# ScalarE fetches 16 table rows per step in three bunches instead of 12 in two; SyncE takes a tile every ten steps instead of eleven

## The chip, the cores and the metric

The kernel runs on one core of one Trainium2 chip. The metric is the device time of one launch in microseconds (us), as the median of several runs. In the names of the profile PE is TensorE (PEld its weight loads), DVE is VectorE, ACT is ScalarE, POOL is GpSimd and SP is SyncE. A name with a q behind it (ACTq, SPq) is the instruction queue of that engine, where instructions are listed that only issue transfers or set registers.

## The reference

The kernel computes a ranking model over 16384 samples in float32. Each sample has 69 item numbers and one label, all of them rows of a table with 100001 rows of 96 floats (384 bytes).

```
u  = emb[batch_user]                 # 16384 x 69 x 96
ql = emb[batch_label[:, 0]]          # 16384 x 96
z  = concat([q, u, q - u, q * u])    # q is ql repeated over the 69 fields
h  = dice(z @ W1 + b1, a1)           # 384 -> 64, dice(x) = (alpha * (1 - p) + p) * x, p = sigmoid(x)
att = (h @ W2 + b2) @ W3 + b3        # 64 -> 16 -> 1
pre = where(batch_user < 100000, u * att, 0)
pooled = einsum("gf,bfe->bge", window, pre)   # ten groups of fields
x = concat([pooled, ql])             # 11 * 96
y = dice(x @ Wf1 ...) -> dice(... @ Wf2 ...) -> ... @ Wf3    # 200, 80, 1
```

What matters here is the first line: 16384 x 69 rows must be fetched from the table by number.

## The kernel before, in words

The samples are worked on in 32 blocks of 512. A block's 512 x 69 items are cut into 69 chunks of 512 items: 64 "main" chunks (eight samples by 64 fields) and five "tail" chunks (512 samples, one of the last five fields each). A chunk is four tiles of 128 rows. Two chunks make a pair, and the kernel's unit of work is the pair: 1104 pairs, one per step of a plan that is written out by hand. `plan[step]` is a list of calls, and the order of the calls is the order in which the instructions stand in each engine's queue; no scheduler moves them.

What one step i does, in the order of the plan:

- sometimes `attend_rows` (every fourth step) and `spread` (every fourth step), which turn hidden values into attention weights;
- `hidden(i - 2)` (L399 and L403 on PE, L405 and L406 on ACT, L407 on DVE): the first layer and its dice;
- `scalar_rows(i, 0)`: a bunch of ScalarE's own row fetches, see below;
- `pool(i - 7)` (the group `acc<-rw,u` on PE, L470 on DVE): the weighted sums over fields;
- `fetch(i)`: for each of the pair's two chunks (j = 0 and 1) four tiles are fetched into the tile `u` and transposed by PE (`ptr<-ident,u`), DVE multiplies them by the label's row (L377), and ACT copies them out (L386, `uT<-ptr`);
- `scalar_rows(i, 1)`: the second bunch.

Beside that, the top layers of a finished block (L502 on PE and what follows) are spread over ten steps of the next block. The last eight steps and the end have an order of their own.

A tile's rows come in one of two ways. The usual one is `gather` (L266): one indirect transfer issued by GpSimd that fetches 128 rows by 128 numbers. The tile `u` has 14 buffers, and a pair's buffer is free when `pool` has read it, seven steps after its fetch.

The other way is the class `Singles`: 196 tiles are fetched row by row, 98 by SyncE and 98 by ScalarE, each row as one transfer of 384 bytes whose address is a register value (L301). Always the last tile (`SLOT = 3`) of a chunk is replaced. `SP_CHUNKS` and `ACT_CHUNKS` say which chunks; such a tile goes to a small ring (four buffers for SyncE, three for ScalarE), and PE waits for it by semaphore. `load` (L286) first loads a group of offsets into registers, 32 at a time on SyncE and 24 at a time on ScalarE. SyncE has nothing else to do and fetches a tile in one go. ScalarE fetches 12 rows in a step, for 11 steps per tile: six rows behind `hidden(i - 2)` (`half == 0`) and six behind `fetch(i)` (`half == 1`). The last of them stand three steps ahead of the step that reads the tile.

Of the kernel before, what the change touches and what calls it, by code (L numbers as in the profile page):

```python
# [48 lines left out]

ROW_BYTES = 4 * E  # L50
SLOT = 3
SP_CHUNKS = [2 * (11 * s + 9) + 1 for s in range(98)]
SP_RING = 4
ACT_CHUNKS = [2 * (11 * s + 15) + 1 for s in range(98)]
ACT_RING = 3
ACT_ROWS = 12
ACT_STEPS = -(-P // ACT_ROWS)
SINGLES = SP_CHUNKS + ACT_CHUNKS
NSB = (len(SINGLES) + P - 1) // P
# [3 lines left out]
def chunk_of(c):  # L63

    n, k = divmod(c, NCH)
    if n == NBLK - 1 and k >= EARLY:
        k = NMAIN + k - EARLY if k < EARLY + NTAIL else k - NTAIL
    return n, k
# [47 lines left out]
def rec_kernel(  # L116
# [158 lines left out]
    class Singles:  # L275
# [19 lines left out]
        def fetch(self, s, start, stop):  # L295

            b, k = self.buffers[s % len(self.buffers)], s % NSEM
            for r in range(start, stop):
                if r % self.group == 0:
                    self.load(s, r)  # L300
                d = self.engine.dma_start(  # L301
                    out=ring[r : r + 1, b], in_=row_bytes[:, bass.ds(self.values[r], ROW_BYTES)]
                ).then_inc(self.sems[k], 16)
                tc.no_tile_sem_insts.add(d.ins.name)
                tc.declare_no_dep(d.ins, group=f"ring{b}", reason="a buffer's readers have waited for its rows")
                fresh.setdefault(b, []).append(d.ins)
            if stop == P:
                for ins in fresh.pop(b):
                    tc.add_to_no_dep_group(f"ring{b}", ins)
                self.given[k] += 16 * P  # L310
                places[self.chunks[s]] = b, self.sems[k], self.given[k]
# [246 lines left out]
    def rows_of(b, n):  # L558
        return lambda: attend_rows(b, n)

    def spread_of(b, n):
        return lambda: spread(b, n)

    def pool_of(k):
        return lambda: pool(k)

    def hidden_of(k):
        return lambda: ys.__setitem__(k, hidden(k, *hs[k]))

    def tails_of(k):  # L570
        def work():
            uT = hs.pop(k)[0]
            for j in range(2):
                if chunk_of(2 * k + j)[1] >= NMAIN:
                    attend_tail(k, j, ys[k], uT)

        return work

    def fetch_of(k, between=()):
        def work():  # L580
            for j in range(2):
                n = chunk_of(2 * k + j)[0]
                if n not in pooled:
                    pooled[n] = bpool.tile([E, G, BLK], F32, tag="pooled", name=f"pooled{n}")
                    pres[n] = xpool.tile([E, NTAIL, BLK], F32, tag="pre", name=f"pre{n}")
            u, uT, quT = fetch(k, lambda: [w() for w in between])
            us[k], hs[k] = u, (uT, quT)

        return work
# [4 lines left out]
    def at(step, *work):  # L594
        plan.setdefault(step, []).extend(work)

    by_sync = Singles("sp", nc.sync, mybir.EngineType.SP, SP_CHUNKS, 0, range(SP_RING), 32)
    for s, m in enumerate(SP_CHUNKS):
        at(max(0, m // 2 - 6), lambda s=s: by_sync.fetch(s, 0, P))

    by_scalar = Singles(
        "act",
        nc.scalar,
        mybir.EngineType.Activation,
        ACT_CHUNKS,
        len(SP_CHUNKS),
        range(SP_RING, SP_RING + ACT_RING),
        2 * ACT_ROWS,
    )
    turn = {}  # L610
    for s, m in enumerate(ACT_CHUNKS):
        for k in range(ACT_STEPS):
            turn.setdefault(m // 2 - 2 - ACT_STEPS + k, []).append((s, k * ACT_ROWS, min(P, (k + 1) * ACT_ROWS)))

    def scalar_rows(i, half):

        for s, start, stop in turn.get(i, []):
            middle = min(stop, start + ACT_ROWS // 2)
            if half == 0:
                by_scalar.fetch(s, start, middle)  # L620
            elif middle < stop:
                by_scalar.fetch(s, middle, stop)

    c = NPAIR - CLOSE
    for i in range(c):
        if i >= 3 and (i - 3) % 4 == 3:
            at(i, rows_of(i - 6, 4))
        if i >= 3:
            at(i, tails_of(i - 3))
        if i >= 4 and (i - 4) % 4 == 3:  # L630
            at(i, spread_of(i - 7, 4))
        if i >= 2:
            at(i, hidden_of(i - 2))
        at(i, lambda i=i: scalar_rows(i, 0))
        if i < c - CLOSE:
            if i >= POOL_LAG:
                at(i, pool_of(i - POOL_LAG))
        else:

            for k in {0: (-15, -14), 1: (-13,), 3: (-12, -11), 4: (-10, -9), 7: (-8, -7)}.get(i - c + 8, ()):  # L640
                at(i, pool_of(c + k))
        at(i, fetch_of(i))
        at(i, lambda i=i: scalar_rows(i, 1))

    at(c, pool_of(c - 6), pool_of(c - 5), tails_of(c - 3), hidden_of(c - 2), fetch_of(c))
    at(c + 1, tails_of(c - 2), hidden_of(c - 1), fetch_of(c + 1))
# [113 lines left out]
```

## Time and profile before

| what | value |
|---|---|
| median of 3 runs | 10986.58 us (10983.78 to 10991.5) |
| the profiled execution's own time | 11010.73 us |
| its span, first to last instruction | 11009.0 us |
| granted TensorE clock, mean | 0.736 |
| gathers on POOL (L266) | 8764 (8636 of tiles `u`, 128 of labels) |
| rows fetched singly (L301) | 12544 on ACT, 12544 on SP |
| POOL busy, PE busy, ACT busy, DVE busy | 8291.3, 8954.4, 3169.5, 3006.0 us |

The busy times count an engine's work on data. Instructions that only issue a transfer or set a register are not counted as busy, so the single rows of ACT and SP (L301) and their offset loads (L286) are in none of these sums; they are seen in the rows of the engine's queue.

### The profile page before, as it was taken

What the parts mean: (1) busy time and instruction counts of PE and PEld (TensorE: products, weight loads), DVE (VectorE), ACT (ScalarE), POOL (GpSimd) and SP (SyncE); (2) the same over time, 40 slices, a digit from 0 to 9 for tenths busy, and PEclk for the clock granted to TensorE, in tenths of its full rate; (3) what the DMA queues carried; (4) which work ended last, traced back from release to release, by engine and by line L of the source; (5) the groups of instructions that cost most, each with busy time, mean ns of one, the idle gap of its engine ahead of it and who ended that gap; (6) DMA issues with size and microseconds to landing.
All of it is one profiled execution on the core that took longest, in us unless ns stands there. A gap on an engine that the chain in (4) does not pass through costs nothing.

```text
span 11009.0 us, 159604 instructions
## 1 busy us (share of the span) xinstructions
PE 8954.4 (81%) x41797; PEld 4357.6 (40%) x41797; DVE 3006.0 (27%) x5327; ACT 3169.5 (29%) x4969; POOL 8291.3 (75%) x8770
## 2 busy tenths in 40 slices
PE   7887888888887888878888878788788888888788
PEld 3333433333443333434433334334334334433335
DVE  3222222222222222222222222222222222222222
ACT  2222222222222222222222222222222222232223
POOL 7777777777777777777777777777777777777776
PEclk6767777677777777777777777777777776777777
DMA  2112111121111211112111121111212112111111
GB/s 49 41 41 43 41 41 41 41 43 41 41 41 41 43 41 41 41 41 43 41 41 41 41 43 41 41 41 41 43 41 41 41 41 43 41 41 41 41 41 35
DMA packets 333393, 457.69 MB, mean 42 GB/s; under 512 B 190594, under 2 KB 191106, under 8 KB 332354
## 3 DMA queue, kind: packets, MB, share of 16 engines
q0 software_dynamic: 280448, 431.33, 18.7%
q1 hardware_dynamic: 26946, 11.28, 0.4%
q10 hardware_dynamic: 25088, 4.87, 0.3%
q8 instruction: 336, 5.51, 0.2%
q14 instruction: 575, 4.71, 0.1%
HBM read 446.74 MB, written 0.07 MB: 41 GB/s over the span
## 4 chain that ended last, share of the span: by engine, by line
POOL 49%; issue 21%; PE 17%; DMA 12%; ACT 0%; DVE 0%; ACTq 0%; POOLq 0%
POOL u L266 48%; DMA u<-in_rows,ids 12%; PE p L502 4%; PE acc L325 3%; PE ph L399 2%; PE ph L403 2%; PE ptr L325 2%; POOL q L266 1%; PE prow L414 1%; PE pa L423 1%; PE ph L396 0%; PE ph L401 0%; PE pc L348 0%; PE patt L431 0%; PE p L513 0%
## 5 line engine op out<-in xcount | busy, mean ns | idle before, releaser
L266 POOL DMA_INDIRECT u<-in_rows,ids x8636 | 8169.4, 946 | 2635.4 <-issue 2429.3
L325 PE MATMUL ptr<-ident,u 128*96 128x128 f32 x8636 | 2015.9, 334 | 1962.7 <-DMA u<-in_rows,ids 1947.6
L386 ACT COPY uT<-ptr 96x512 f32<-96x512 f32 x2208 | 1267.4, 582 | 4384.7 <-DVE quT L377 3221.7
L325 PEld LDWEIGHTS ptr<-ident,u 128*96 128x96 f32 x8636 | 1154.4, 150 | 2736.8 <-DMA u<-in_rows,ids 2299.9
L325 PEld LDWEIGHTS acc<-rw,u 128*96 128x96 f32 x16018 | 1700.9, 189 | 1200.9 <-issue 1023.8
L407 DVE TENSOR_TENSOR y<-ph,y 128x512 f32<-128x512 f32 x1104 | 763.4, 691 | 4867.9 <-ACT y L406 4691.3
L377 DVE TENSOR_TENSOR quT<-ptr,qT 96x512 f32<-96x512 f32 x2048 | 1372.4, 677 | 1969.8 <-PE ptr L325 1967.9
L325 PE MATMUL acc<-rw,u 128*96 128x20 f32 x16018 | 1807.5, 260 | 37.5 <-DVE rw L436 31.8
L399 PE MATMUL ph<-uT,A 128*64 128x512 f32 x4096 | 1662.9, 889 | 1.0 <-ACT uT L386 1.0
L403 PE MATMUL ph<-quT,wn 96*64 96x512 f32 x4416 | 1601.4, 797 | 0.0
L405 ACT ACTIVATE y<-ph 128x512 f32<-128x512 f32 x1104 | 659.1, 597 | 2692.8 <-PE ph L403 2660.9
L406 ACT ACTIVATE y<-y,wn,na1c 128x512 f32<-128x512 f32 x1104 | 898.1, 814 | 37.2
L403 PEld LDWEIGHTS ph<-quT,wn 96*64 96x64 f32 x4416 | 441.1, 189 | 1050.7 <-issue 1049.6
L502 PE MATMUL p<-pooled,wf 96*100 96x512 f32 (+1 forms) x1400 | 679.4, 633 | 0.0
L399 PEld LDWEIGHTS ph<-uT,A 128*64 128x64 f32 x4096 | 266.0, 177 | 616.8 <-issue 612.1
L470 DVE COPY pooled<-acc 96x160 f32<-96x160 f32 x1008 | 420.6, 417 | 133.4 <-PE acc L325 133.4
L414 PE MATMUL prow<-y,v 128*32 128x512 f32 x2208 | 454.7, 900 | 1.0 <-DVE y L407 1.0
L502 PE MATMUL p<-pre,V 96*100 96x512 f32 (+1 forms) x700 | 401.3, 720 | 3.7 <-DVE x L485 3.4
L502 PEld LDWEIGHTS p<-pooled,wf 96*100 96x100 f32 x1400 | 256.1, 195 | 327.6 <-issue 327.6
L436 DVE SCALAR_TENSOR_TENSOR rw<-patt,bb,wn 128x320 f32<-128x320 f32 x554 | 277.5, 542 | 210.1 <-PE patt L431 206.6
L416 ACT COPY row<-prow 128x512 f32<-128x512 f32 (+1 forms) x277 | 161.9, 584 | 432.5 <-PE prow L414 402.1
L431 PE MATMUL patt<-ident,row 128*128 128x128 f32 x1108 | 221.6, 336 | 16.4 <-DVE pre L424 14.9
(72 smaller groups left out, 2438.5 us busy)
## 6 DMA issues: line engine op xcount, KB each, us to landing
ring<-in_rows SPq DMA_DIRECT2D x12544, 0.4 KB
ring<-in_rows ACTq DMA_DIRECT2D x12544, 0.4 KB
u<-in_rows,ids POOLq DMA_INDIRECT x8636
ids<-in_idx SPq DMA_DIRECT2D x8, 560.0 KB, 3.8
q<-in_emb,ids POOLq DMA_INDIRECT x128
wf<-in_far SPq DMA_DIRECT2D x1, 1209.0 KB, 6.4
wn<-in_near SPq DMA_DIRECT2D x1, 236.0 KB, 3.7
ids<-in_idx SPq DMA_DIRECT2D x1, 140.0 KB, 2.2
```

What stands on the lines that cost most here:

```text
L266: nc.gpsimd.indirect_dma_start(out=dst, out_offset=None, in_=table, in_offset=bass.IndirectOffsetOnAxis(ap=index, axis=0),)
L325: ins = op(out, ring[:, at[0]].bitcast(F32) if at else u[:, 4 * (c % 2) + t, :], other, **how)
L377: nc.vector.tensor_tensor(quT[:, j, :].rearrange("e (s f) -> e s f", f=FM), ptr.rearrange("e (s f) -> e s f", f=FM), by_field(q[:, k * NS ...
L386: nc.scalar.copy(uT[j][0:E], ptr)
L399: nc.tensor.matmul(p, As[n % 2][:, k // 4, :], uT[j], start=True, stop=False)
L403: nc.tensor.matmul(p, Wp, quT[:, j, :], start=False, stop=True)
L405: nc.scalar.activation(y, ph, AF.Sigmoid, scale=S_DICE)
L406: nc.scalar.activation(y, y, AF.Identity, bias=a1c, scale=na1c)
L407: nc.vector.tensor_mul(y, ph, y)
L414: nc.tensor.matmul(pr[32 * k : 32 * (k + 1), :], v2, ys[b + k], start=True, stop=True)
L470: nc.vector.tensor_copy(pooled[n][:, :, k * NS : (k + 2) * NS].rearrange("e g s -> e s g"), pa.rearrange("e j s g -> e (j s) g"),)
L502: nc.tensor.matmul(p1, w[:, h * DH : (h + 1) * DH], x, start=(k == 0), stop=(k == KTOP - 1))
```

## The change

ScalarE fetches 16 rows in a step instead of 12, so a tile takes eight steps instead of eleven, and it takes a tile every eight steps: 136 tiles instead of 98. Its tiles are now the last tile of the first chunk of a pair (j = 0) and no longer of the second. The 16 rows stand in three bunches: five behind `hidden(i - 2)`, five between the two chunks of `fetch(i)` (thus between the two copies of L386), and six behind `fetch(i)`. The loads of offsets grow with `2 * ACT_ROWS` from 24 to 32 values. SyncE takes a tile every ten steps instead of eleven: 109 tiles instead of 98. The rings, the gathers that remain and everything else stay.

```diff
-SP_CHUNKS = [2 * (11 * s + 9) + 1 for s in range(98)]
+SP_CHUNKS = [2 * (10 * s + 8) + 1 for s in range(109)]
 SP_RING = 4
-ACT_CHUNKS = [2 * (11 * s + 15) + 1 for s in range(98)]
+ACT_CHUNKS = [2 * (8 * s + 11) for s in range(136)]
 ACT_RING = 3
-ACT_ROWS = 12
+ACT_ROWS = 16
...
-    def scalar_rows(i, half):
+    def scalar_rows(i, third):
 
         for s, start, stop in turn.get(i, []):
-            middle = min(stop, start + ACT_ROWS // 2)
-            if half == 0:
-                by_scalar.fetch(s, start, middle)
-            elif middle < stop:
-                by_scalar.fetch(s, middle, stop)
+            by_scalar.fetch(s, start + third * ACT_ROWS // 3, start + (third + 1) * ACT_ROWS // 3)
...
-        at(i, fetch_of(i))
-        at(i, lambda i=i: scalar_rows(i, 1))
+        at(i, fetch_of(i, [lambda i=i: scalar_rows(i, 1)]))
+        at(i, lambda i=i: scalar_rows(i, 2))
```

## The prediction

> **What bounds the kernel now.** I read the page's busy times first, then who waited for whom on POOL and on PE, then the end of the chain. The page has PE busiest, but the waits say otherwise:
>
> ```profile
> PE 8954.4 (81%) x41797; PEld 4357.6 (40%) x41797; DVE 3006.0 (27%) x5327; ACT 3169.5 (29%) x4969; POOL 8291.3 (75%) x8770
> L266 POOL DMA_INDIRECT u<-in_rows,ids x8636 | 8169.4, 946 | 2635.4 <-issue 2429.3
> POOL u L266 <- issue: 2429.3, 7961, 0.3
> POOL u L266 <- PE ptr L325: 49.8, 163, 0.3
> PE ptr L325 <- DMA u<-in_rows,ids: 1947.6, 2358, 2.8
> PE acc L325 <- DVE rw L436: 31.8, 27, 3.0
> ```
>
> In the waits the numbers are us in total, times, longest. No gather waited longer than 0.3 us, and it did so before nearly every one: this is the gap of POOL's own issue. So a gather costs 0.946 us of work and 0.305 us (2635.4/8636) of gap, 1.251 us, and 8764 of them fill 10964 us: the first starts at 3.3 us, the last at 10967.05, a straight line. PE, in contrast, stood 1948 us waiting for gathered rows. POOL sets the pace and PE follows. (The chain of waits gives PE 17%; where it leaves POOL the gap is the same 0.3 us, so nothing was lost there.) The end of the chain:
>
> ```profile
> 10965.80 0.95 POOL u L266
> 10966.75 0.30 issue
> 10967.05 2.54 DMA u<-in_rows,ids
> 10969.59 0.04 issue
> 10969.63 0.32 PE ptr L325
> ```
>
> The last gather is followed by 42 us of PE, DVE and ACT work, which the change leaves alone. Time = 3.3 + 1.251 x gathers + 42.
>
> **The change part by part.**
>
> *Fewer gathers.* 109 + 136 tiles instead of 98 + 98 are 49 more outside POOL: 8715 gathers. Saved: 49 x 1.251 = 61.3 us, on the bound itself. In the profiled execution, span 11009.0, own time 11010.73, this gives 10949.4. The median is 24 us (0.22%) below that execution, so I scale: 61.2 us off 10986.6, 10925.4.
>
> *More rows on ACT: 136 x 128 = 17408, 4864 more.* They are covered by ACT's idle time, if it is long enough. The rows that price them:
>
> ```profile
> L301 ACTq DMA_DIRECT2D ring<-in_rows x12544: 213/213/566, 36.6 to 10740.7; - x200
> L286 ACTq TENSOR_LOAD <-offsets x588: 717/1678/1739, 34.8 to 10737.4; - x196
> L286 SPq TENSOR_LOAD <-offsets x392: 2023/2176/2396, 4.0 to 10309.1; - x196
> 5009.80 0.60 ACT L405 ACTIVATE y<-ph 128x512 f32<-128x512 f32 x1 [4.78 <-PE ph L403]
> 5010.43 0.81 ACT L406 ACTIVATE y<-y,wn,na1c 128x512 f32<-128x512 f32 x1
> 5012.25 2.01 ACTq L301 DMA_DIRECT2D ring<-in_rows  x6
> 5014.30 1.23 ACT L386 COPY uT<-ptr 96x512 f32<-96x512 f32 x2 [3.06 <-DVE quT L377]
> 5015.02 1.74 ACTq L301 DMA_DIRECT2D ring<-in_rows  x6
> 5017.62 0.60 ACT L405 ACTIVATE y<-ph 128x512 f32<-128x512 f32 x1 [2.09 <-PE ph L403]
> ```
>
> (Durations in ns are least/median/greatest; of the timeline, start and length in us.) Six rows take 1.74 us from the first one's start to the last one's end: 5 steps plus 0.213, so 0.305 us a row. Where SP issues too it is more; over the trace the mean distance of rows within a bunch is 0.326. A load of 32 offsets is priced by SP's row, 2.18 us, plus 0.25 because the first row behind a load takes 0.45 to 0.49 instead of 0.213.
>
> What ACT needs if it never waits for data, for two steps with one load: L406 stands behind L405 by 0.63, then its queue goes on while L406 and the copies run. Before: 2 x 0.63 + 1.68 + 0.25 + 24 x 0.305 = 10.5, or 5.3 us a step. After: 2 x 0.63 + 2.18 + 0.25 + 32 x 0.305 = 13.4, or 6.7 us. A step lasts 8715/1104 x 1.251 = 9.88 us. Even with nothing overlapped, ACT's sum is 3170 + 17408 x 0.326 + 544 x 2.43 = 10167 us of about 10950. So in the mean ACT keeps pace.
>
> [...]
>
> *What ACT's added time does to PE.* It adds 4 x 0.326 + 0.27 (loads: 544 x 2.43 less 98 x (5 x 1.68 + 0.72 + 6 x 0.25), over 1088 steps) = 1.6 us a step. At best nothing of it reaches PE. At worst all does, in 1088 steps: 1710 us, still below the 1948 us that PE waits for rows. The catch-up stretch above shows which is nearer: PE, behind by one step, went from one `pool` at 5009.69 to the next at 5017.49, 7.8 us, and ACT still waited 0.8 us for PE before the last L405. With 6.7 needed against 7.8, I take nearly nothing. The bunch between the two copies delays the second copy by up to 1.5 us; what is late next is PE's second transpose of the following step, a step away, and the hidden layer that reads `uT` two steps later.
>
> *How late may PE be?* POOL stalls only when `u` has no free buffer: 14 buffers, released seven steps after the fetch, so about 70 us. From the starts of the gathers and their transposes in the trace I worked out PE's lag: 2.5 us at least, 6.8 at the 75th percentile, at most 18.1 in blocks 0 to 30, and 32.5 at 10758 us in the last block. There remain 37 us.
>
> *The end.* There the lag counts directly: it falls from 23.7 us around 10843 to 3.0 at the last gathers, just in time. In the last 20 steps two or three tiles more are single (steps 1083, 1088, 1091; before, the last was at 1082), which brings POOL ahead of PE by 2.5 to 3.8 us, and ACT's rows now last to step 1088. Where PE doesn't follow, that part of the gain is lost, and up to 5 us more for ACT. Zero to 9 us; I take 2, because PE still waited 3.5 us for rows behind 10920.
>
> *At nothing:* SP's 1408 more rows. A tile takes some 50 us (74 rows in 29.22 us), every 99 us instead of 109; SP waited 5144 us for ring buffers. The ids that it loads on the same queue, 50 steps ahead, stay ahead. ACT's ring is read seven steps before its buffer is filled again (8(s-3)+18 against 8s+1), where it was 13. The queues' packets took 0.4% and 0.3% of the engines. The gather's pace has been 1.251 in the last 60 us too, where no rows are issued, so rows don't slow it. 49 more waits on PE are for tiles due two steps earlier.
>
> Sum: 10986.6 - 61.2 + 2 = 10927.
>
> **The rivals.** *PE's lag eats the gain in part.* If ACT's bunches add their full 1.6 us in the 20 steps of the last block where PE is behind, the lag there is 32 + 32 = 64 us, near the 70, and the end comes 10 to 30 us later: 10937 to 10957. Against it stands the 0.8 us of idle ACT in the catch-up stretch. *No gain:* PE becomes the bound everywhere. This needs over 1950 us of new waits on PE, more than everything that ACT adds; time 10965 to 11008. *Slower: ACT becomes the bound,* through the price of a row. Two queues issue closer together, and a row is slower when they meet (up to 0.566 us). [...] For it: the mean, 0.326, is above the quiet 0.305. Against: the waits of L386 and L405, 3222 and 2661 us before. *That the change doesn't reach POOL* is excluded by its count: 4 x 2208 - 245 + 128 = 8715.
>
> **How the numbers follow.** The forecast 0.80 (10920 to 10937), the partial gain 0.08, no gain 0.04, slower 0.08. The range holds the forecast's and most of the partial case: 10919 to 10948. About 0.2% is what a measurement of this kernel can tell from no change, 22 us. Faster 0.88, same 0.04, slower 0.08.
>
> **What would show it.** After: 8636 - 49 = 8587 gathers of `u`, 1.251 us apart, none with a wait over 0.3 us, span near 10950; 17408 and 13952 rows; ACT's rows still near 0.31 to 0.33 apart; PE still waiting over 1000 us for gathered rows, ACT's waits before L386 and L405 shorter by about 1500 together. Wrong if POOL waits for PE by whole microseconds, if PE waits for L386 instead of gathers, or if the tail behind the last gather is longer than 42 us by more than ten.

## The result and the profile after

The changed kernel takes 10925.1 us (median of 4 runs, 10924.09 to 10926.21), the kernel before 10987.9 us beside it: a ratio of 0.9943 with a 95% interval of 0.9926 to 0.996, or 62.8 us less (by the interval 44 to 81). The prediction was 10927, in a range of 10919 to 10948.

The busy times, the gathers and the last waits on POOL and PE (us in total, times, longest), of the changed kernel's profile:

```profile
span 10924.5 us, 172151 instructions
PE 8916.8 (82%) x41797; PEld 4347.4 (40%) x41797; DVE 2997.8 (27%) x5327; ACT 3181.0 (29%) x4969; POOL 8225.3 (75%) x8721
L266 POOL DMA_INDIRECT u<-in_rows,ids x8587 | 8103.7, 944 | 2619.7 <-issue 2455.0
POOL u L266 <- issue: 2455.0, 8047, 0.3
POOL u L266 <- PE ptr L325: 56.1, 184, 0.3
PE ptr L325 <- DMA u<-in_rows,ids: 1864.9, 2296, 2.7
PE acc L325 <- DVE rw L436: 41.9, 27, 4.6
PE ptr L325 <- ACT uT L386: 14.3, 17, 2.5
```

There are 49 gathers fewer, and still none of them waits over 0.3 us: POOL remains the bound and makes no pause but the 0.3 us ahead of each gather. PE waits 1865 us for gathered rows, 83 us less than before, and 14.3 us for ACT's copies. The added work on ACT, whose busy time does not show it, is in the rows of its queue (ns, least/median/greatest):

```profile
L301 ACTq DMA_DIRECT2D ring<-in_rows x17408: 213/213/527, 23.8 to 10747.0; - x198
L286 ACTq TENSOR_LOAD <-offsets x544: 2123/2182/2230, 21.5 to 10733.4; - x182
```

A row costs what it cost (a median of 213 ns in both profiles), and a load of 32 offsets costs on ACT what SP's row of before had shown (2182 ns against 2176). The three bunches in the timeline of ACT (start and length in us), in a step where the queue is behind:

```profile
8012.23 0.81 ACT L406 ACTIVATE y<-y,wn,na1c 128x512 f32<-128x512 f32 x1
8014.56 1.66 ACTq L301 DMA_DIRECT2D ring<-in_rows  x5
8016.26 0.58 ACT L386 COPY uT<-ptr 96x512 f32<-96x512 f32 x1 [3.22 <-issue]
8016.33 1.43 ACTq L301 DMA_DIRECT2D ring<-in_rows  x5
8017.80 0.58 ACT L386 COPY uT<-ptr 96x512 f32<-96x512 f32 x1 [0.96 <-issue]
8017.88 1.73 ACTq L301 DMA_DIRECT2D ring<-in_rows  x6
```

Between L406 and the first row stands the load of offsets (2.18 us, not listed among these lines). Both copies wait for "issue": PE had transposed their data by 8013.92, and the queue is still loading offsets and handing out rows. That is the price of the change on ACT, and little of it comes through to PE: the 14.3 us above.

The end of the span against the one before, in windows of the trace from the start of the last gather to the end of the span (us of the window, busy time and count of PE, PEld, DVE, ACT and POOL, the granted TensorE clock, DMA share, GB/s); first before, then after:

```profile
10967.10:11009.00 41.90, 34.63 (x227) 28.97 (x225) 7.22 (x18) 9.14 (x18) 0.90 (x1) 0.78 0.02 5
```

```profile
10885.40:10924.50 39.10, 32.63 (x231) 25.97 (x227) 7.18 (x18) 9.13 (x18) 0.94 (x1) 0.82 0.02 5
```

The tail became 2.8 us shorter with nearly the same instructions, at a higher granted clock (0.82, before 0.78).

### The profile page after: what moved, and what is told of

It reads as the page before. It is cut to its first block, busy times and chain, and to the rows that moved or that the text cites. A ratio compares the mean times of both kernels' runs of the same rounds, so it can differ in the third digit from the quotient of the medians.

```text
span 10924.5 us, 172151 instructions
## 1 busy us (share of the span) xinstructions
PE 8916.8 (82%) x41797; PEld 4347.4 (40%) x41797; DVE 2997.8 (27%) x5327; ACT 3181.0 (29%) x4969; POOL 8225.3 (75%) x8721
## 4 chain that ended last, share of the span: by engine, by line
POOL 51%; issue 23%; PE 15%; DMA 9%; ACT 1%; DVE 0%; ACTq 0%; POOLq 0%; DVEq 0%
POOL u L266 50%; DMA u<-in_rows,ids 9%; PE p L502 4%; PE acc L325 3%; PE ph L403 2%; PE ph L399 2%; PE ptr L325 2%; POOL q L266 1%; PE prow L414 1%; PE ph L396 0%; PE ph L401 0%; PE pa L423 0%; PE pc L348 0%; PE patt L431 0%; ACTq L301 0%
## 5 line engine op out<-in xcount | busy, mean ns | idle before, releaser
L386 ACT COPY uT<-ptr 96x512 f32<-96x512 f32 x2208 | 1283.4, 581 | 4630.3 <-DVE quT L377 2969.4
L325 PE MATMUL acc<-rw,u 128*96 128x20 f32 x15930 | 1812.3, 259 | 52.0 <-DVE rw L436 41.9
L405 ACT ACTIVATE y<-ph 128x512 f32<-128x512 f32 x1104 | 658.5, 596 | 2401.0 <-PE ph L403 2283.5
L406 ACT ACTIVATE y<-y,wn,na1c 128x512 f32<-128x512 f32 x1104 | 898.2, 814 | 36.7
L416 ACT COPY row<-prow 128x512 f32<-128x512 f32 (+1 forms) x277 | 161.6, 583 | 413.1 <-PE prow L414 305.4
```

Source lines behind the costliest of these rows:

```text
L325: ins = op(out, ring[:, at[0]].bitcast(F32) if at else u[:, 4 * (c % 2) + t, :], other, **how)
L386: nc.scalar.copy(uT[j][0:E], ptr)
L405: nc.scalar.activation(y, ph, AF.Sigmoid, scale=S_DICE)
L406: nc.scalar.activation(y, y, AF.Identity, bias=a1c, scale=na1c)
```

## The experiments

The theory of all of them: the time is 3.3 us, plus 1.249 us for each gather, plus a tail of about 40 us, as long as ScalarE, SyncE and PE keep pace. The rivals say that the added rows cost something, or that the bunches' places matter, or that the mean hides a bound that is near. Each kernel was timed beside the kernel before; differences below are against that run of before (10986.9 us in the first group, 10991.0 in the second, 10987.4 in the last).

**SyncE's part alone.**

```diff
-SP_CHUNKS = [2 * (11 * s + 9) + 1 for s in range(98)]
+SP_CHUNKS = [2 * (10 * s + 8) + 1 for s in range(109)]
-ACT_CHUNKS = [2 * (11 * s + 15) + 1 for s in range(98)]
+ACT_CHUNKS = [2 * (11 * s + 15) for s in range(98)]
```

> SyncE's part alone: a tile every ten steps (109 tiles), ScalarE as before (98 tiles, 12 rows in two bunches), but its tiles moved to the first chunk of the pair so that no tile is taken twice. 207 single tiles, 8753 gathers. Theory (the time is 3.3 us + 1.249 us x gathers + a tail of about 40 us, whatever fetches the other tiles): 11 gathers fewer, 13.7 us faster than before, about 10974. Rival (SyncE's denser rows slow the gathers or ScalarE's rows, where both issue): a gain clearly below 13.7, gathers more than 1.249 us apart.

Measured: 10973.5 us, 13.5 less, ratio 0.9987 (0.9977 to 0.9996). The gathers stand 1.249 us apart. The theory's 13.7 us is met to 0.2 us, closer than the interval (4 to 25 us less) can vouch for. (The second edit only moves ScalarE's tiles to the first chunk of the pair, so that no tile is taken twice.)

**ScalarE's part alone.** The changed kernel with SyncE's old line:

```diff
-SP_CHUNKS = [2 * (10 * s + 8) + 1 for s in range(109)]
+SP_CHUNKS = [2 * (11 * s + 9) + 1 for s in range(98)]
```

> ScalarE's part alone: 16 rows in three bunches, 136 tiles, SyncE as before (98). 234 single tiles, 8726 gathers. Theory: 38 gathers fewer, 47.4 us faster than before, about 10940. Rival (ScalarE's rows cost something that the larger saving hides): a gain clearly below 47, with POOL waits over 0.3 us or a longer tail behind the last gather.

Measured: 10940.3 us, 46.7 less, ratio 0.9956 (0.9939 to 0.9972). The two parts add up: 13.5 + 46.7 = 60.2 beside 62.8 and, in this group, 61.3 for the whole (the two-bunch form below).

**The rows without the gain.** In the changed kernel's `fetch`:

```diff
+AGAIN = set(SINGLES[::5])
...
                 if single(2 * i + j, t):
                     wait_for_single(2 * i + j, t)
-                else:
+                if not single(2 * i + j, t) or 2 * i + j in AGAIN:
                     gather(rows, u[:, 4 * j + t, :], ids[n][:, 4 * k + t : 4 * k + t + 1])
```

> The changed kernel with every fifth of its 245 single tiles gathered by GpSimd as well (into the place in u that nobody reads then): all the added rows, loads and bunches stay, and the number of gathers is again that of before, 8764. Theory (only the number of gathers counts, rows are free): the time of before, within 5 us of 10988. Rival (rows have a price that the change paid out of its 61 us): slower than before by that price; if ScalarE's added 1.6 us per step reached the path in the last block alone, by 10 to 30 us.

Measured: 10988.0 us, 1.0 more than before, ratio 1.0 (0.9991 to 1.001). The page's row of the gathers (a line was added, so it is L267 here):

```profile
L267 POOL DMA_INDIRECT u<-in_rows,ids x8636 | 8150.8, 944 | 2634.4 <-issue 2341.6
```

The number of gathers is that of before, and so is the time, with 6272 more rows in the queues. So the rows are free to within what this comparison can tell, some 10 us.

**Two bunches of eight.** The old `scalar_rows(i, half)` with `ACT_ROWS = 16`:

```diff
-        at(i, fetch_of(i, [lambda i=i: scalar_rows(i, 1)]))
-        at(i, lambda i=i: scalar_rows(i, 2))
+        at(i, fetch_of(i))
+        at(i, lambda i=i: scalar_rows(i, 1))
```

> The changed kernel, but ScalarE's 16 rows in two bunches of eight, behind hidden and behind fetch, as the 12 stood before, and none between the two copies. 8715 gathers. Theory (ScalarE has room, so the bunches' places do not matter to the time): 10925, the time of the changed kernel, with PE's lag behind the gathers at most a few us different. Rival (three bunches are what makes 16 rows affordable): slower than the changed kernel by 10 us or more, through L386 or L405 being late and a longer tail.

Measured: 10925.6 us, ratio to before 0.9943 (0.9927 to 0.996), the time of the three bunches. The largest lag of PE behind the gathers, worked out from the trace as in the prediction, is 26.5 us, with three bunches 26.8. At 16 rows a step the third bunch changes nothing that can be seen.

**ScalarE at 22 rows a step.** Here and below a third page of offsets takes 512 bytes per partition, and to make room for it SyncE's ring was given three buffers of 384 instead of four. Where a tile is not a whole number of steps (6 x 22 is more than 128), `scalar_rows` also cuts the last step short; that edit is left out below.

```diff
-SP_RING = 4
-ACT_CHUNKS = [2 * (8 * s + 11) for s in range(136)]
+SP_RING = 3
+ACT_CHUNKS = [2 * (6 * s + 9) for s in range(181)]
-ACT_ROWS = 16
+ACT_ROWS = 22
...
-        2 * ACT_ROWS,
+        32,
```

> ScalarE pushed further: 22 rows per step in three bunches (7, 7, 8), a tile every six steps (181 tiles), offsets still loaded 32 at a time; SyncE as in the changed kernel (109 tiles). SyncE's ring has three buffers instead of four, to make room for the longer table of offsets. 8670 gathers, 45 fewer than the changed kernel. By the prediction's sum ScalarE needs 0.63 + 22 x 0.324 + 22/32 x 2.43 = 9.4 us a step (9.0 at the quiet price of 0.305), and a step of POOL lasts 9.8. Theory (ScalarE still just keeps pace): 56 us faster than the changed kernel, 10869. Rival (the bunches fit in the mean but not in the steps with more work on ScalarE, so PE's lag grows to the end of u's buffers): POOL shows waits of whole microseconds, and the gain is below 40 us or gone.

Measured: 10874.2 us, 116.8 less than before (94 gathers fewer than before are 117.4), ratio 0.9894 (0.9877 to 0.991). PE's waits show how close ACT has come:

```profile
PE ptr L325 <- DMA u<-in_rows,ids: 769.8, 964, 2.0
PE ptr L325 <- ACT uT L386: 569.7, 358, 4.4
```

PE's wait for gathered rows is 770 us where the changed kernel had 1865: more than half of its spare time is gone, and its wait for ACT's copies rose from 14 to 570 us. POOL still never waits over 0.3 us for PE; PE's lag reaches 38.0 us of the 70.

**ScalarE at 26 rows a step.** The ring and the loads are as with 22 rows.

```diff
-ACT_CHUNKS = [2 * (8 * s + 11) for s in range(136)]
+ACT_CHUNKS = [2 * (5 * s + 8) for s in range(217)]
-ACT_ROWS = 16
+ACT_ROWS = 26
```

> ScalarE pushed past the point where the prediction's sum makes it the bound: 26 rows per step, a tile every five steps (217 tiles), the rest as with 22 rows. 8634 gathers. The sum is 0.63 + 26 x (0.305 to 0.324) + 26/32 x 2.43 = 10.5 to 11.0 us a step, more than POOL's 9.77. Theory (a row's price, not its number of bytes, decides when ScalarE becomes the bound): ScalarE sets the pace, 11400 to 11950 us, its waits before L386 and L405 nearly gone, and POOL waits for PE. Rival (ScalarE's queue hides more than the sum allows): 10825, POOL still without a wait.

Measured: 12355.6 us, ratio 1.1242 (1.1219 to 1.1264). The waits of POOL and PE:

```profile
POOL u L266 <- PE ptr L325: 1096.3, 432, 17.0
POOL u L266 <- PE acc L325: 559.6, 136, 13.7
PE ptr L325 <- ACT uT L386: 1541.4, 875, 6.2
```

PE's waits for gathered rows are nearly gone (27.9 us), PE waits for ACT, and POOL waits for PE, by up to 17 us at a time. PE's lag has a median of 75 us over most of the run, near the prediction's 70 us of buffers: `u` has none free. The mechanism is the one expected; the size is 400 us above the expected 11400 to 11950. A step took 12355.6/1104 = 11.2 us where the sum gave 10.5 to 11.0. The sum left out ACT's smaller work (L416, the top layers' dice L483 and L484, L349). Counted from the trace, the time in which ACT works or its queue hands something out is 10.5 us a step without that work, the low end of the sum, and 10.8 with it. For the other 0.4 us ACT stood still; why was not followed up.

**SyncE at a tile every six steps.**

```diff
-SP_CHUNKS = [2 * (10 * s + 8) + 1 for s in range(109)]
-SP_RING = 4
+SP_CHUNKS = [2 * (6 * s + 8) + 1 for s in range(181)]
+SP_RING = 3
```

> SyncE pushed: a tile every six steps instead of ten (181 tiles), ring of three buffers; ScalarE as in the changed kernel (136 tiles). 8643 gathers, 72 fewer than the changed kernel. SyncE needs about 50 us a tile of the 59 us that six steps last. Theory (only the number of gathers counts): 90 us faster than the changed kernel, 10835. Rival (two queues of single rows get in each other's way: rows of ScalarE at more than 0.33 us, or SyncE's tiles late, so that PE waits for the ring): clearly less than 90.

Measured: 10841.2 us, 149.8 less than before (121 gathers fewer are 151.1), ratio 0.9865 (0.9848 to 0.9881). SyncE is the cheaper place for more tiles: beside its rows and their offsets its queue has only the loads of item numbers and the stores of the result.

**Both.** The lines of the last and of the 22 rows together.

> Both pushed: ScalarE 22 rows per step and a tile every six steps (181 tiles), SyncE a tile every six steps (181 tiles), rings of three buffers each. 8598 gathers. Theory: 146 us faster than the changed kernel, 10779. Rival: where rows of both queues meet they cost more than 0.324, and ScalarE's sum (9.4 of 9.72 us per step) has no room for it: from 0.34 us a row on ScalarE is the bound, and the gain is smaller than that of SyncE's part alone (10835).

Measured: 10854.1 us, ratio 0.9872 (0.9855 to 0.9888): 12.9 us slower than SyncE's part alone, with 45 gathers fewer. The theory (10779) fails by 75 us, and the rival's sign came. Waits of POOL and PE, and the window behind the last gather:

```profile
POOL u L266 <- PE ptr L325: 66.2, 141, 6.7
PE ptr L325 <- ACT uT L386: 961.1, 535, 4.4
10771.40:10856.80 85.40, 72.17 (x468) 50.47 (x466) 23.65 (x49) 24.70 (x43) 0.91 (x1) 0.83 0.01 3
```

The gathers finished early, at 10771 us, but the last transpose began 50.7 us behind the last gather, where 2.5 us is usual. ACT had hardly any room left (0.63 + 22 x 0.334 + 1.67 = 9.6 us of a step of 9.72, before its smaller work). PE fell behind over the whole run, from a median lag of 9 us in the first sixteenth of the gathers to 58 in the last, and what it was behind is paid in the tail.

**19 rows a step, with SyncE every six steps and every five and a half.** The loads of offsets are as with 22 rows.

```diff
-SP_CHUNKS = [2 * (10 * s + 8) + 1 for s in range(109)]
-SP_RING = 4
-ACT_CHUNKS = [2 * (8 * s + 11) for s in range(136)]
+SP_CHUNKS = [2 * (6 * s + 8) + 1 for s in range(181)]       # the other: 2 * (11 * s // 2 + 8) + 1, 197 tiles
+SP_RING = 3
+ACT_CHUNKS = [2 * (7 * s + 10) for s in range(155)]
-ACT_ROWS = 16
+ACT_ROWS = 19
```

> ScalarE at 19 rows per step (6, 6, 7), a tile every seven steps (155 tiles), and SyncE a tile every six steps (181 tiles), rings of three buffers. 8624 gathers. ScalarE's sum is 0.63 + 19 x 0.33 + 19/32 x 2.43 = 8.3 us of a step of 9.75, where 22 rows needed 9.5 of 9.72 and left no room. Theory: 19 gathers fewer than SyncE's part pushed alone (10841), 10817, POOL without a wait over 0.3 us, a tail behind the last gather of about 40 us. Rival (ScalarE's last steps make PE late at the end even with room in the mean): a tail of 45 to 85 us, so no gain over 10841.

> As the one with 19 rows per step, and SyncE a tile every five and a half steps (197 tiles). 8608 gathers. SyncE needs 51 us a tile of the 53.5 us that its steps last. Theory: 16 gathers fewer again, 10797. Rival (SyncE is now the late one: PE waits for the ring's tiles, and with rows of both queues meeting all the time ScalarE's rows cost more): PE shows waits at L325 for rows of the ring, and the time is above 10817.

Measured: 15848.8 and 16582.6 us, but the kernel before took 13552.4 us on that chip, so neither theory can be judged by these two runs. The rows of the queues in the first of them:

```profile
L301 SPq MOVE ring<-in_rows x23168: 1/29/1481, 6.7 to 15644.5; - x200
L301 ACTq MOVE ring<-in_rows x19840: 2/29/1473, 99.7 to 15616.4; - x199
```

A register move of a row, which takes 30 ns at most in the traces from other chips, took up to 1.48 us there. Both kernels were run again on another chip.

> The kernel with 19 rows per step on ScalarE and a SyncE tile every six steps again, because in its first run the kernel before took 13552 us beside it, 2560 more than in every other comparison, so that nothing can be read from it about the gathers. 8624 gathers. Theory: beside a kernel before at 10987, 10817. Rival (the loss lies in the kernel, not in that chip): over 10987 here too.

> The kernel with 19 rows per step on ScalarE and a SyncE tile every five and a half steps again, for the same reason. 8608 gathers. Theory: 10797. Rival (SyncE's 51 us a tile do not fit 53.5 where both queues meet): PE waits for rows of the ring, above 10817.

Measured: 10815.2 us (ratio 0.9843, 0.9826 to 0.9859) and 10795.9 us (ratio 0.9827, 0.981 to 0.9843), 172.2 and 191.5 us less than before; the theory has 140 x 1.249 = 174.8 and 156 x 1.249 = 194.8. PE's waits in the second one:

```profile
PE ptr L325 <- DMA u<-in_rows,ids: 1669.9, 2006, 3.1
PE ptr L325 <- ACT uT L386: 71.5, 59, 4.9
```

PE waits for gathers again and hardly for ACT, so three rows a step fewer than 22 (and a tile every seven steps) give ACT its room back. The version with 19 rows and 5.5 steps is the fastest of all that were tried, 1.2% below the changed kernel.

## Why the prediction was right, point by point

*POOL sets the pace.* Shown: in every kernel in which ACT had room, and even with 22 rows, the median follows the number of gathers to within 3.3 us, from 11 to 156 fewer, and giving the 49 gathers back gave the time back.

*61.2 us for 49 gathers.* Right. The page of before has gathers of 946 ns and that of after 944. Over 8764 gathers 2.24 ns (945.98 less 943.74, from the trace) are 20 us, most of the 24 us by which the profiled execution of before stood above its median. So this part of the difference between the two profiled spans (84.5 us) belongs to no edit; scaling to the median was the right step.

*ACT's added rows are hidden.* Right, and shown to some 10 us by the run with the rows but without the gain. The price was right too: 0.324 us from row to row within bunches against the 0.326 used. One reading of the prediction was off: the longest row, 0.566 us, is a first row behind a load of offsets, where 0.448 is usual, and not only two queues meeting. In the changed kernel rows that overlap one of SyncE's follow each other after 0.314 us on average, others after 0.307 (distances under 0.42 us).

*The point from which ACT decides.* With nothing overlapped, ACT's busy time of before (3170 us) and 544 loads of offsets at 2.43 us (1322 us) leave (10926 - 3170 - 1322)/17408 = 0.37 us a row at 16 rows a step, an estimate from before's profile and the changed kernel's counts. Turned round, at 0.324 us a row, the runs put it between 22 and 26 rows a step (sums of 9.4 and 11.0 us against about 9.8), and where SyncE's rows are dense too, at 22. At 26 rows the time was 3% above the top of the range from the sum and 8% above its bottom. Counted from the traces, ACT was working or its queue handing out (pauses under 0.1 us included) for 60% of the span before, 71% in the changed kernel, 82% with 19 rows and SyncE every five and a half steps, 93% with 22 rows, 94% with 22 rows and SyncE every six steps, and 97% with 26. ACT's busy time on the page stood at 3140 to 3180 us all the while.

*The end.* This term was mis-sized: 2 us of loss were taken, with up to 9 possible, and the trace shows none. (The time alone could not tell 2 us from nothing.) PE's last transpose starts 2.50 us behind the last gather, before 2.58. PE's lag in the last block even fell, from 32.5 to 26.8 us at most. The tail is 2.8 us shorter, and over the runs in which PE is not late at the end its length goes with the granted clock in it: 43.7 us at 0.73, 42.0 at 0.75, 41.9 at 0.78, 39.1 at 0.82, 38.5 at 0.85, 36.5 at 0.92. The step that failed is the one that let the lag of before's profile carry over. The other kernels in which ACT had room show 23.5 to 30.3 us, and the 23.5 is of SyncE's part alone, in which ACT has its old 12 rows. So the 32.5 us was probably that one execution's (its granted clock was 0.59 from 10750 to 10800 us, where the lag is greatest); no second one of before was profiled.

*What would show it.* The count of gathers, the rows and PE's wait came as written; the gathers stood 1.249 us apart and not 1.251, and the span was 10924.5 us and not near 10950, both mostly by the faster gather above. One sign did not come: ACT's waits before L386 and L405 were to fall by 1500 us together. By name they fell by 630 (L386 for DVE from 3221.7 to 2969.4, L405 for PE from 2660.9 to 2283.5), and L386's wait for "issue" rose from 826.9 to 1282.6; first before, then after:

```profile
ACT uT L386 <- DVE quT L377: 3221.7, 1491, 7.6
ACT y L405 <- PE ph L403: 2660.9, 1033, 10.5
ACT uT L386 <- issue: 826.9, 269, 3.5
```

```profile
ACT uT L386 <- DVE quT L377: 2969.4, 1434, 7.0
ACT y L405 <- PE ph L403: 2283.5, 926, 9.1
ACT uT L386 <- issue: 1282.6, 561, 3.6
```

The profile counts the time of a row in ACT's queue as idle time of the engine, under the name of what came last, so the added rows need not shorten a wait. What the sign was meant to show is there all the same: the time in which ACT neither worked nor handed anything out fell from 4442 to 3123 us, by 1319.

## What to carry to other kernels

Ask which engine never pauses, count its instructions, and price a change by how many it takes away; the busiest engine of the page need not be it (here PE with 82% of the span, against POOL's 75%). An engine whose busy time is low may still be full (ACT with 26 rows a step was busy for a quarter of the span and filled 97% of it): add what its queue issues (rows, loads, register moves) by the distance from one to the next, and leave room for what the sum forgets. Here a sum of 8.3 us in a step of 9.75 was enough, and one of 9.6 in 9.72 was not. A queue with little other work, such as SyncE's here, should be filled first.

## What the runs showed of the hardware that was not expected

- The gather showed two speeds: 946 ns on average in the profiled executions of before and of the first kernel with 19 rows when it was run again, 944 ns (943.4 to 944.6) in all others. It goes with the execution and not with the kernel, as far as two cases can show: both profiled executions were some 25 us longer than the median of their kernel (11010.7 against 10986.6, 10841.4 against 10815.2), and 2.2 to 2.4 ns for each gather are 20 us of that. This is a third of what the change brought.
- On one chip all three kernels were slow: the kernel before by 23% (13552 against 10987), the kernels with 19 rows by 47% and 54% (15849 against 10815, 16583 against 10796). There register moves took up to 1.48 us in the two traces; of before none was kept from there. The two kernels with more small instructions (43008 and 45056 single rows against 25088) lost more. What held the queues up was not found, nor whether it is the chip's or that hour's.
- The granted TensorE clock in the last 40 us ranged from 0.73 to 0.92 between kernels that do the same work there, which goes with a difference of 7 us. What sets it was not tried.
